# A convolutional attention block with linear attention and routed experts: where the output bias is added, where the experts' row comparisons and the routing exponentials are queued, and one branch

## The chip, the cores and the metric

The kernel runs on one core of one Trainium2 chip, all in float32 except where the profile says otherwise. The metric is the time of one execution on the device, in microseconds (us); less is better. TensorE is called PE, VectorE DVE, ScalarE ACT, GpSimd POOL and SyncE SP, as in the profile. PEld is the weight load of PE, which lies beside the matmuls.

## What is computed

The input `x` has the shape 2 x 256 x 56 x 56: two images, 256 channels (C). There are two layers, each with residual sums. Layer 1 works on 6272 tokens, which are 49 blocks of 128; block 24 holds the end of image 0 and the beginning of image 1.

```python
x = x + conv_attention(group_norm(x))       # layer 0: 1x1 conv to q,k,v; depthwise 3x3;
                                            # 7x7 neighbourhood attention, dilation 1 and 2; projection
t = tokens(x)                               # layer 1
t = t + linear_attention(layer_norm(t))     # below
t = t + experts(layer_norm(t))              # below
out = images(t)

# linear attention of tokens x
Q, K = elu(x @ Wq) + 1, elu(x @ Wk) + 1
KV = einsum('nshd,nshv->nhdv', K, x @ Wv)
msg = einsum('nlhd,nhdv,nlh->nlhv', Q, KV, Z) @ Wm          # Z: one over Q times the sum of K
h = relu(concat(x, layer_norm(msg, g1, b1)) @ W1) @ W2
return x + layer_norm(h, g2, b2)                            # b2 is the output bias of the change

# experts: top 2 of 8, hidden width 1024
probs = softmax(x @ Wr + br);  top_p, top_idx = top_k(probs, 2)
weights = top_p / top_p.sum()
y_e = gelu((norm(x) * ln_g[e] + ln_b[e]) @ W1[e] + b1[e]) @ W2[e] + b2[e]
return sum of weights * y_e over the two chosen experts
```

## The kernel before, in words

**Stages.** (1) Attention of image 0 and the convolutions. (2) The linear attention of the first half of the tokens (`linear(..., 0)`): first the stage of the keys (`keys`, L267), pair of blocks by pair of blocks, then queries, messages (`message`, L1906), feed-forward and routing (`route`, L2028) of the groups of four blocks, which run about 530 to 745 us from the start; convolution work for image 1 fills in. (3) Attention of image 1 (`Attention`, L606), with the first expert tiles run beside it, about 765 to 1030 us. (4) The linear attention of the second half (`linear(..., 1)`), with expert tiles up to number 13 beside it, to about 1440 us. (5) The remaining full expert tiles and five half tiles, to about 1970 us. (6) The last tokens are read back, transposed and written.

**Experts.** The router scatters every token's row of 256 values, with its index and its two weights, into a DRAM buffer `xs`, sorted by expert (`scatter`, L168, an indirect DMA of POOL). A tile is 256 rows of one expert. `fetch` (L1534) reads the tile's rows into `xr` and the expert's weights into `w1e` and `w2e`, and works out four small DVE results from the rows: `eq` (L1557, which row is in use; L1560 and L1561 make it the row's weight) and `idi` (L1559, the row's token as an integer); `so` and `sv` (L1563, L1567) come from the expert's number alone. `turn` (L1570) transposes the rows with PE (`px`), scales them on DVE (`xe`, L1579) and prepares `yt`, the expert's bias times the weight, on POOL (L1589). `run` (L1591) is a generator: it fetches tile t+1, does the eight hidden parts of tile t (matmuls `ph` L1607, Gelu on ACT L1611), calls `turn` for tile t+1, does the second matmuls `py` (L1625), adds them to `yt` (L1631, DVE, with `eq`) and scatters `yt` into `y` by `idi`. Each `next` of the generator is a step; the other stages place the steps between their own work.

**What sets the order.** PE's order is written out by hand: it is the order of the program (`manual_schedule`). The orders of all other engines and of the DMA queues are made by a planner before the kernel runs. It simulates the kernel and gives each engine, when it comes free, the instruction of highest priority whose inputs it takes as there; the priority is the place in the program, unless `high_priority` is given. `tc.issue_after(ins)` puts what is written under it behind `ins` on that engine. The engines execute their streams in the order planned.

**The lines that the change and the prediction touch.** `keys`: the tokens `t` of a pair are normalised into `xt` (which goes to PE), then `t` is overwritten on ACT by its scaled form (L296), and POOL adds the output bias `b2` in place (L299, 128 x 512); `t` is not read again until the feed-forward's residual. `rstd` (L257) computes a reciprocal square root with DVE L261 and POOL `pow` L262, at high priority; `message` calls it for every two blocks. `weights` (L2018): the `Exp` of the routing (L2021), then DVE lines L2022 to L2026. It is called by `route` after the matmuls L2083 and L2084, which count how many rows each expert has had and take `chosen` (L2074) and `before` (L2076) from DVE. Attention: the scores `s_ps` (L651), their Exp on ACT (L655), the product with the bias table on DVE (`p`, L656), the values `po` on PE (L665). In the second half the string list `parts` (L2303) orders the steps row by row; `e` is one expert step, and it does nothing once tile 13 is done. L2389 to L2395: `ex.more` says whether an expert has more tiles than are provided for; then the code in `If` runs. The last reads are L2340, by SP and ACT, the transposes `pto` L2352, and L2406 to L2413 are a branch to a general version, not taken here.

Of the kernel before, what the change touches and what calls it, by code (L numbers as in the profile page):

```python
# [13 lines left out]
F32 = mybir.dt.float32  # L14
AF = mybir.ActivationFunctionType
# [30 lines left out]
E = 8  # L46
# [80 lines left out]
def hybrid_kernel(ctx: ExitStack, tc: tile.TileContext, a: dict, out: bass.AP):  # L127
# [49 lines left out]
    newest = [None, None, None]  # L177
# [89 lines left out]
    def keys(tk, wk, sm, ps, bank, w_k, b2, kx, acc, n0, n, p, first, last, eager):  # L267
# [31 lines left out]
        nc.gpsimd.tensor_tensor(t, t, b2[p].unsqueeze(1).to_broadcast([rows, n, C]), ALU.add)  # L299
# [1054 lines left out]
    class Experts:  # L1354
# [179 lines left out]
        def fetch(self, t, nh, pools):  # L1534
# [20 lines left out]
            x.eq = self.small.tile([P, 2], F32, name="eq")  # L1555
            eq = x.eq[:, :nh]
            nc.vector.tensor_scalar(eq, xr[:, :, C + 3], tab.etm[:, k : k + 1], None, ALU.is_equal)  # L1557
            x.idi = self.small.tile([P, 2], mybir.dt.int32, name="idi", bufs=4)
            nc.vector.tensor_copy(x.idi[:, :nh], xr[:, :, C])  # L1559
            nc.vector.tensor_tensor(eq, eq, xr[:, :, C + 2], ALU.mult)  # L1560
            nc.vector.tensor_tensor(eq, eq, xr[:, :, C + 1], ALU.add)  # L1561
# [6 lines left out]
            return x  # L1568

        def turn(self, x, pools):  # L1570
# [7 lines left out]
            for ct in range(2):  # L1578
                newest[0] = nc.vector.tensor_scalar(  # L1579
                    x.xe[:, ct, :], px[:, ct, :nh, :].rearrange("p j t -> p (j t)"),  # L1580
                    x.sv[:, ct : ct + 1], x.sv[:, 2 + ct : 3 + ct], ALU.mult, ALU.add,
                ).ins
            b2 = pools.b2e()
# [7 lines left out]
        def run(self, ts, pools, between=lambda i: None):  # L1591
# [7 lines left out]
            for i, (t, nh) in enumerate(ts):  # L1599
# [4 lines left out]
                for j in range(NJ):  # L1604
                    p1 = pools.ph()[:, : nh * P]
                    for ct in range(2):
                        nc.tensor.matmul(  # L1607
                            p1, x.w1[:, ct, j * P : (j + 1) * P], x.xe[:, ct, :],
                            start=(ct == 0), stop=(ct == 1),
                        )  # L1610
                    nc.scalar.activation(hT[:, j, :], p1, AF.Gelu, bias=x.sv[:, 4 + j : 5 + j])  # L1611
                    if j % 2:
                        yield
# [33 lines left out]
    def linear(ph, tk, half, behind=None):  # L1647
# [258 lines left out]
        def message(n0, n, qz, out):  # L1906
# [3 lines left out]
            for k0 in range(0, n, 2):  # L1910
                pm = ps_h.tile([P, 2, C], F32, name="pm", tag="h")
# [106 lines left out]
        def weights(rt, ms, row, n):  # L2018

            r = rt.sm.tile([P, 4], F32, name="rsum")[:, :n]  # L2020
            nc.scalar.activation(ms[1], ms[1], AF.Exp)  # L2021
# [95 lines left out]
        def all_keys():  # L2117
# [58 lines left out]
    def layer1(whole, tk, conv_ctx=None, conv=None, behind=None):  # L2176
# [3 lines left out]
        conv = conv or none  # L2180

# [66 lines left out]
        def experts():  # L2248
# [7 lines left out]
            turn=lambda: tc.issue_after(newest[1]),  # L2256
            xr=lambda: xc.tile([P, 2, XW], F32, name="xr"),
# [27 lines left out]
        with ExitStack() as ph:  # L2285
            ln = linear(ph, tk, 1)
            pools.px = lambda: ln.ps_a.tile([P, 2, 2, P], F32, name="px", tag="a")
# [6 lines left out]
            with tc.manual_schedule(engines={mybir.EngineType.PE}):  # L2294
                for i, _ in enumerate(ln.keys()):
# [11 lines left out]
                    "fefepefefereePfePeree", "eepeereePeePeree", "eeepePe",  # L2307
# [7 lines left out]
        with ExitStack() as ph:  # L2315
# [10 lines left out]
                turn=nullcontext,  # L2326
                xr=lambda: xp.tile([P, 2, XW], F32, name="xr"),
# [56 lines left out]
            with tc.manual_schedule(engines={mybir.EngineType.PE}):  # L2384
# [15 lines left out]
    with ExitStack() as ph:  # L2400
# [6 lines left out]
        bad[0:1, 0:1], min_val=0, max_val=1, skip_runtime_bounds_check_because="a comparison's result"  # L2407
# [42 lines left out]
```

## Time and profile before

| what | value |
|---|---|
| median of 3 runs | 1992.35 us (1986.69 to 1992.89) |
| the profiled execution's own time | 1992.68 us |
| its span, first to last instruction | 1990.9 us |
| PE busy | 1840.8 us (92%) |
| DVE / ACT / POOL busy | 1092.3 / 705.9 / 584.9 us |
| mean granted PE clock | 0.970 |

All times of the trace count from the start of the span; 1.8 us of the execution's own time lie outside it. A line of the timeline gives the start, the duration, the engine, the line of the kernel, the operation, its output and inputs with their shape, the number of instructions put together, and in brackets how long the engine had been idle before it and what released it. A line of the windows gives a stretch, its length, the busy time and number of instructions of PE, PEld, DVE, ACT and POOL, the granted PE clock, the busy share of the DMA engines and GB/s.

### The profile page before, as it was taken

The numbers are of one execution on the slowest core, as the hardware profiler recorded it, in microseconds if no ns is written. First come the engines' busy times: TensorE is split into PE (matmuls) and PEld (weight loads), VectorE is DVE, ScalarE is ACT, GpSimd is POOL, SyncE is SP. The second block draws the span as 40 slices with busy tenths as digits, with TensorE's granted clock in tenths as the row PEclk, the third lists the DMA queues.
The fourth block names the chain that finished last, engine by engine and source line by source line (L and its number), as shares of the span: only waits on it lengthen the run. The fifth ranks groups of instructions, "written<-read, shape, count | busy, mean of one in ns | idle before, by whom it ended". The sixth has DMA issues, their size and how long they took to land.

```text
span 1990.9 us, 27720 instructions
## 1 busy us (share of the span) xinstructions
PE 1840.8 (92%) x9996; PEld 1306.9 (66%) x9996; DVE 1092.3 (55%) x2727; ACT 705.9 (35%) x1337; POOL 584.9 (29%) x634
## 2 busy tenths in 40 slices
PE   6999899988899997999989989999899999999996
PEld 3544454556555654666668756577788888888885
DVE  6887988889897646465547334555532212121221
ACT  2333324334433323545536443323322222323332
POOL 4630132025102344111126311445422222222221
PEclk9999899999999995999999999999999999999998
DMA  4753422350014235664474110115477676767995
GB/s 113 158 131 114 141 86 80 93 167 17 25 43 111 84 86 179 161 160 125 130 199 130 56 35 32 50 59 150 147 227 201 190 199 190 199 190 196 297 282 164
DMA packets 200152, 268.85 MB, mean 135 GB/s; under 512 B 30952, under 2 KB 158614, under 8 KB 199760
## 3 DMA queue, kind: packets, MB, share of 16 engines
q1 hardware_dynamic: 167920, 223.95, 37.6%
q0 software_dynamic: 19728, 27.54, 7.5%
q10 hardware_dynamic: 12352, 15.43, 2.3%
q8 instruction: 83, 1.36, 0.3%
q14 instruction: 69, 0.57, 0.1%
HBM read 200.19 MB, written 70.95 MB: 136 GB/s over the span
## 4 chain that ended last, share of the span: by engine, by line
PE 49%; DMA 4%; DVE 3%; ACT 3%; issue 1%; POOL 1%; SPq 0%; ACTq 0%; DVEq 0%; POOLq 0%
PE py L1625 13%; PE ph L1607 13%; PE p L1946 4%; PE x L1625 2%; PE x L1607 2%; DMA y<-yt,idi 2%; PE py L1962 2%; PE po L665 2%; DMA xr<-xs 1%; PE pm L1916 1%; PE kx L316 1%; PE x L358 1%; PE kp L304 1%; PE s_ps L651 1%; PE pq L1876 1%; PE px L1576 1%
## 5 line engine op out<-in xcount | busy, mean ns | idle before, releaser
L1607 PE MATMUL ph<-xe,w1e 128*128 128x256 f32 (+1 forms) x1448 | 311.3, 371 | 12.8 <-ACT hT L1611 7.9
L1625 PE MATMUL py<-w2e,hT 128*128 128x256 f32 x1392 | 311.4, 380 | 0.0
L1611 ACT ACTIVATE hT<-ph,sv 128x256 f32<-128x256 f32 (+1 forms) x362 | 165.6, 462 | 390.1 <-PE ph L1607 377.3
L1607 PEld LDWEIGHTS ph<-xe,w1e 128*128 128x128 f32 x1448 | 262.7, 191 | 52.0 <-ACT hT L1611 10.1
L1625 PEld LDWEIGHTS py<-w2e,hT 128*128 128x128 f32 x1392 | 260.3, 190 | 33.0 <-issue 0.2
L168 POOL DMA_INDIRECT y<-yt,idi x101 | 160.2, 1587 | 326.7 <-DVE yt L1631 188.7
L578 DVE SCALAR_TENSOR_TENSOR yc<-ypad,w,yc 128x1120 f32<-128x1120 f32 x144 | 202.5, 1410 | 28.4 <-ACT yc L568 26.0
L262 POOL TENSOR_TENSOR rs<-rs,mhalf 128x2 f32<-128x2 f32 (+3 forms) x90 | 72.8, 812 | 324.1 <-DVE rs L261 276.0
L528 PE MATMUL py<-x_sb,wq 128*128 128x448 f32 (+1 forms) x384 | 154.2, 533 | 7.2 <-ACT ypad L534 5.6
L655 ACT ACTIVATE p<-s_ps 112x952 f32<-112x952 f32 (+5 forms) x88 | 102.1, 1160 | 150.6 <-PE s_ps L651 101.4
L1559 DVE CAST idi<-xr 128x2 int32<-128x2 f32 (+1 forms) x53 | 10.1, 191 | 255.1 <-DMA xr<-xs 255.1
L656 DVE TENSOR_TENSOR p<-p,tab 112x952 f32<-112x952 f32 (+5 forms) x88 | 122.0, 1389 | 48.6 <-ACT p L655 41.3
L549 PE MATMUL pc<-ypad,diag 128*128 128x448 f32 x324 | 131.4, 547 | 0.0
L1631 DVE SCALAR_TENSOR_TENSOR yt<-py,eq,yt 128x256 f32<-128x256 f32 x87 | 41.8, 482 | 156.6 <-PE py L1625 156.5
L1589 POOL TENSOR_SCALAR yt<-b2e,eq 128x256 f32<-128x256 f32 x101 | 52.2, 522 | 253.5 <-DMA b2e<-in_L_ffn_b 214.9
L168 POOL DMA_INDIRECT xs<-row,si x98 | 97.5, 995 | 70.2 <-DVE si L2092 40.2
L528 PEld LDWEIGHTS py<-x_sb,wq 128*128 128x128 f32 x384 | 71.7, 197 | 69.4 <-issue 55.5
L571 DVE SCALAR_TENSOR_TENSOR yc<-ypad,w,yc 128x784 f32<-128x784 f32 x96 | 104.9, 1113 | 1.3 <-ACT yc L568 0.9
L665 PE MATMUL po<-p,v 98*32 98x170 f32 (+5 forms) x960 | 71.1, 378 | 30.3 <-DVE p L656 15.5
L549 PEld LDWEIGHTS pc<-ypad,diag 128*128 128x128 f32 x324 | 60.0, 191 | 52.3 <-issue 48.5
L1946 PE MATMUL p<-m2T,fw 128*128 128x512 f32 (+2 forms) x224 | 93.8, 542 | 0.0
L1946 PE MATMUL p<-xT,fw 128*128 128x512 f32 (+1 forms) x208 | 92.7, 568 | 0.0
(392 smaller groups left out, 2889.0 us busy)
## 6 DMA issues: line engine op xcount, KB each, us to landing
w1e<-in_L_ffn_W SPq DMA_DIRECT2D x53, 1024.0 KB
w2e<-in_L_ffn_W SPq DMA_DIRECT2D x53, 1024.0 KB
yd<-yc SPq DMA_DIRECT2D x24, 784.0 KB
ld<-yd SPq DMA_DIRECT2D x28, 448.0 KB
xr<-xs SPq DMA_DIRECT2D x48, 260.0 KB
b2e<-in_L_ffn_b SPq DMA_DIRECT2D x53, 128.0 KB
t<-td SPq DMA_DIRECT2D x12, 512.0 KB
y<-t ACTq DMA_DIRECT2D x24, 256.0 KB
```

Of the source, the lines that this page charges most:

```text
L168: ins = nc.gpsimd.indirect_dma_start(out=dst[:, :], out_offset=bass.IndirectOffsetOnAxis(ap=index, axis=0), in_=src, in_offset=None, **kw,)
L528: nc.tensor.matmul(py[:, :n, :], self.wq1[:, ct, oc * P : (oc + 1) * P], self.x_sb[:, ct, (q0 + g0) * WW : (q0 + g0 + n) * WW], start=(ct ...
L549: nc.tensor.matmul(pc, diag[:, tap, :], ypad[:, dy : dy + SHARE, dx : dx + WW], start=(tap == 0), stop=(tap == 8),)
L571: nc.vector.scalar_tensor_tensor(yc[:, y0:y1, :], src, w, yc[:, y0:y1, :], ALU.mult, ALU.add)
L578: nc.vector.scalar_tensor_tensor(yc[:, y0:y1, :], src, w, yc[:, y0:y1, :], ALU.mult, ALU.add)
L655: nc.scalar.activation(p[:nk, :, :n], s_ps[:nk, :, :n], AF.Exp)
L656: nc.vector.tensor_tensor(grid(p), grid(p), table[:nk], ALU.mult)
L665: nc.tensor.matmul(dst[hs] if w is None else den[hs], v[:nk, hs] if w is None else w[:nk, :], p[:, h, :, o : o + q.shape[2]], start=first ...
L1607: nc.tensor.matmul(p1, x.w1[:, ct, j * P : (j + 1) * P], x.xe[:, ct, :], start=(ct == 0), stop=(ct == 1),)
L1611: nc.scalar.activation(hT[:, j, :], p1, AF.Gelu, bias=x.sv[:, 4 + j : 5 + j])
L1625: nc.tensor.matmul(py, hT[:, j, h * P : (h + 1) * P], x.w2[:, j, :], start=(j == 0), stop=(j == NJ - 1),)
L1946: nc.tensor.matmul(p1[:, :w], fw1[:, k, oc * P : (oc + 1) * P], rhs, start=(k == 0), stop=(k == 3))
```

## The change

Five edits. (1) `keys` gets no bias for the full pairs of the first half, so 12 of its 24 POOL additions of 128 x 512 leave it; `message` in the first half adds the bias instead, at the head of each pass over two blocks. The single block 24 keeps its addition in `keys`. (2) The four DVE lines that need `xr` become `weigh`; for tiles fetched while `pools.beside` is true (the attention of image 1) it is called in `turn`, after `xe`, and otherwise in `fetch` as before. (3) The last Gelu written so far is remembered, and in the second half the Exp of `weights` is queued behind it on ACT. (4) The last two strings of `parts` get one and two letters `e` more at their head. (5) In the ordinary run the `If` on `more`, with its code, is gone; `more` is merged into `bad` with one DVE operation, so the general version would take care of it.

```diff
--- before.py
+++ after.py
@@ -174,7 +174,7 @@
 
     evac_n = [0]
 
-    newest = [None, None, None]
+    newest = [None, None, None, None]
 
     def evac(dst, src):
 
@@ -296,7 +296,8 @@
             nc.scalar.activation(
                 t[:, k, :], t[:, k, :], AF.Identity, bias=up[:, 1, k : k + 1], scale=up[:, 0, k : k + 1]
             )
-        nc.gpsimd.tensor_tensor(t, t, b2[p].unsqueeze(1).to_broadcast([rows, n, C]), ALU.add)
+        if b2 is not None:
+            nc.gpsimd.tensor_tensor(t, t, b2[p].unsqueeze(1).to_broadcast([rows, n, C]), ALU.add)
         yield
         kps = bank()[p]
         for k in range(n):
@@ -1552,20 +1553,27 @@
                 x.w2, a["L1_ffn_W2"][bass.ds(e, 1)].rearrange("one (j p) d -> p (one j) d", p=P)
             )
             x.e = e
+            x.etm, x.eq = tab.etm[:, k : k + 1], None
+            if not pools.beside:
+                self.weigh(x)
+            so = self.small.tile([P, 4 + NJ, E], F32, name="so")
+            nc.vector.tensor_tensor(
+                so, self.sel, tab.oh[:, k, :].unsqueeze(1).to_broadcast([P, 4 + NJ, E]), ALU.mult
+            )
+            x.sv = self.small.tile([P, 4 + NJ], F32, name="sv")
+            nc.vector.tensor_reduce(x.sv, so, AX.X, ALU.add)
+            return x
+
+        def weigh(self, x):
+
+            xr, nh = x.xr, x.nh
             x.eq = self.small.tile([P, 2], F32, name="eq")
             eq = x.eq[:, :nh]
-            nc.vector.tensor_scalar(eq, xr[:, :, C + 3], tab.etm[:, k : k + 1], None, ALU.is_equal)
+            nc.vector.tensor_scalar(eq, xr[:, :, C + 3], x.etm, None, ALU.is_equal)
             x.idi = self.small.tile([P, 2], mybir.dt.int32, name="idi", bufs=4)
             nc.vector.tensor_copy(x.idi[:, :nh], xr[:, :, C])
             nc.vector.tensor_tensor(eq, eq, xr[:, :, C + 2], ALU.mult)
             nc.vector.tensor_tensor(eq, eq, xr[:, :, C + 1], ALU.add)
-            so = self.small.tile([P, 4 + NJ, E], F32, name="so")
-            nc.vector.tensor_tensor(
-                so, self.sel, tab.oh[:, k, :].unsqueeze(1).to_broadcast([P, 4 + NJ, E]), ALU.mult
-            )
-            x.sv = self.small.tile([P, 4 + NJ], F32, name="sv")
-            nc.vector.tensor_reduce(x.sv, so, AX.X, ALU.add)
-            return x
 
         def turn(self, x, pools):
 
@@ -1580,6 +1588,8 @@
                     x.xe[:, ct, :], px[:, ct, :nh, :].rearrange("p j t -> p (j t)"),
                     x.sv[:, ct : ct + 1], x.sv[:, 2 + ct : 3 + ct], ALU.mult, ALU.add,
                 ).ins
+            if x.eq is None:
+                self.weigh(x)
             b2 = pools.b2e()
             nc.sync.dma_start(
                 b2, a["L1_ffn_b2"][bass.ds(x.e, 1)].rearrange("one d -> (one d)").partition_broadcast(P)
@@ -1608,7 +1618,9 @@
                             p1, x.w1[:, ct, j * P : (j + 1) * P], x.xe[:, ct, :],
                             start=(ct == 0), stop=(ct == 1),
                         )
-                    nc.scalar.activation(hT[:, j, :], p1, AF.Gelu, bias=x.sv[:, 4 + j : 5 + j])
+                    newest[3] = nc.scalar.activation(
+                        hT[:, j, :], p1, AF.Gelu, bias=x.sv[:, 4 + j : 5 + j]
+                    ).ins
                     if j % 2:
                         yield
                 between(i)
@@ -1908,6 +1920,9 @@
             mns = []
             ss = sm.tile([P, 4], F32, name="ssm")
             for k0 in range(0, n, 2):
+                if half == 0:
+                    tt = tk.at(n0 + k0, 2)
+                    nc.gpsimd.tensor_tensor(tt, tt, b2.unsqueeze(1).to_broadcast([P, 2, C]), ALU.add)
                 pm = ps_h.tile([P, 2, C], F32, name="pm", tag="h")
                 for k in range(min(2, n - k0)):
                     for b, c0, c1 in parts(n0, n):
@@ -2018,7 +2033,8 @@
         def weights(rt, ms, row, n):
 
             r = rt.sm.tile([P, 4], F32, name="rsum")[:, :n]
-            nc.scalar.activation(ms[1], ms[1], AF.Exp)
+            with tc.issue_after(newest[3]) if half and newest[3] is not None else nullcontext():
+                nc.scalar.activation(ms[1], ms[1], AF.Exp)
             nc.vector.tensor_scalar(r, ms[1], 1.0, None, ALU.add)
             nc.vector.reciprocal(r, r)
             nc.vector.tensor_tensor(row[:, :n, C + 1], ms[1], r, ALU.mult)
@@ -2126,7 +2142,7 @@
                     j = i - k
                     if j == i and j < len(pairs):
                         live[j] = keys(
-                            tk, wk, sm, ps_a, bank, w_k, b2, kx, acc, *pairs[j], j == 0, j == len(pairs) - 1, j < 3 and half == 0
+                            tk, wk, sm, ps_a, bank, w_k, b2 if half or pairs[j][1] == 1 else None, kx, acc, *pairs[j], j == 0, j == len(pairs) - 1, j < 3 and half == 0
                         )
                     if 0 <= j < len(pairs):
                         next(live[j])
@@ -2178,6 +2194,7 @@
 
         run = tk.run
         conv = conv or none
+        newest[3] = None
 
         def fill(n=1):
             for _ in range(n):
@@ -2254,6 +2271,7 @@
         xc = experts() if run else None
         pools = SimpleNamespace(
             turn=lambda: tc.issue_after(newest[1]),
+            beside=run == 0,
             xr=lambda: xc.tile([P, 2, XW], F32, name="xr"),
             xe=lambda: xc.tile([P, 2, ST], F32, name="xe"),
             yt=lambda: xc.tile([P, 2, C], F32, name="yt"),
@@ -2284,6 +2302,7 @@
 
         with ExitStack() as ph:
             ln = linear(ph, tk, 1)
+            pools.beside = False
             pools.px = lambda: ln.ps_a.tile([P, 2, 2, P], F32, name="px", tag="a")
             pools.ph = lambda: ln.ps_q.tile([P, 2, ST], F32, name="ph", tag="q")[:, 0, :]
             summed = []
@@ -2304,7 +2323,7 @@
                     "qewexewexqwexqq", "meqemeq", "meqfmqfeffff",
                     "mqfpPPPPfmqfrfrff", "mqfpPPPPfmqfrfrff", "mqfpPPPPfmqfrfrff",
                     "mqfpcfmfqrfPPfPrPef", "meqefepfmfqPPrPfPerefe", "mefefpfmferePPfePerPee",
-                    "fefepefefereePfePeree", "eepeereePeePeree", "eeepePe",
+                    "fefepefefereePfePeree", "eeepeereePeePeree", "eeeeepePe",
                 )
                 for part in steps(ln, order[early1:], parts, {"e": tiles, "w": merging, "x": prepared}):
                     if part == "c":
@@ -2324,6 +2343,7 @@
             ps_t = ph.enter_context(tc.tile_pool(name="p4pt", bufs=2, space=PSUM, reuse_waits="tile"))
             pools = SimpleNamespace(
                 turn=nullcontext,
+                beside=False,
                 xr=lambda: xp.tile([P, 2, XW], F32, name="xr"),
                 xe=lambda: xp.tile([P, 2, ST], F32, name="xe"),
                 yt=lambda: xp.tile([P, 2, C], F32, name="yt"),
@@ -2386,13 +2406,16 @@
                 for i, _ in enumerate(ex.run(slots, pools, between)):
                     for _ in range((i > 2) + (2 < i < 12)):
                         chunk(work)
-            more = nc.values_load(
-                ex.more[0:1, 0:1], min_val=0, max_val=NTL,
-                skip_runtime_bounds_check_because="the number of tiles is bounded by the counts",
-            )
-            with tc.If(more > 0):
-                for _ in ex.run([(t, 2) for t in range(NFS, NTL)] + [(k, 1) for k in range(NHS, E)], pools):
-                    pass
+            if run == 0:
+                nc.vector.tensor_tensor(bad, bad, ex.more[0:1, 0:1], ALU.max)
+            else:
+                more = nc.values_load(
+                    ex.more[0:1, 0:1], min_val=0, max_val=NTL,
+                    skip_runtime_bounds_check_because="the number of tiles is bounded by the counts",
+                )
+                with tc.If(more > 0):
+                    for _ in ex.run([(t, 2) for t in range(NFS, NTL)] + [(k, 1) for k in range(NHS, E)], pools):
+                        pass
             last = [read(n0, n, False) for n0, n in order[early2:]]
             for h in held + last:
                 write(*h, (nc.scalar, nc.sync), [(ps_t, "pt"), (ps_h, "ph")])
@@ -2404,7 +2427,8 @@
         rest = first_image(conv, ph)
         layer1(ph, tokens, conv_ctx, rest, anchors["residual4"])
     bad = nc.values_load(
-        bad[0:1, 0:1], min_val=0, max_val=1, skip_runtime_bounds_check_because="a comparison's result"
+        bad[0:1, 0:1], min_val=0, max_val=NTL,
+        skip_runtime_bounds_check_because="a comparison's result or a number of tiles",
     )
     with tc.If(bad > 0):
         with ExitStack() as ph:
```

More of the change, by code (lines that the diff above doesn't have):

```diff
@@ L1554, in fetch @@
             x.e = e
[L1555 to L1561, printed above, removed]
+            x.etm, x.eq = tab.etm[:, k : k + 1], None
+            if not pools.beside:
+                self.weigh(x)
             so = self.small.tile([P, 4 + NJ, E], F32, name="so")
@@ L1568, in fetch @@
             return x
+        def weigh(self, x):
+            xr, nh = x.xr, x.nh
+            x.eq = self.small.tile([P, 2], F32, name="eq")
+            eq = x.eq[:, :nh]
+            nc.vector.tensor_scalar(eq, xr[:, :, C + 3], x.etm, None, ALU.is_equal)
+            x.idi = self.small.tile([P, 2], mybir.dt.int32, name="idi", bufs=4)
+            nc.vector.tensor_copy(x.idi[:, :nh], xr[:, :, C])
+            nc.vector.tensor_tensor(eq, eq, xr[:, :, C + 2], ALU.mult)
+            nc.vector.tensor_tensor(eq, eq, xr[:, :, C + 1], ALU.add)
         def turn(self, x, pools):
```

## The prediction

> **What bounds the kernel now.** I read the totals first, then the slices, then the stretches by stage, then the stalls of PE one by one.
>
> ```profile
> PE 1840.8 (92%) x9996; PEld 1306.9 (66%) x9996; DVE 1092.3 (55%) x2727; ACT 705.9 (35%) x1337; POOL 584.9 (29%) x634
> PE   6999899988899997999989989999899999999996
> PEclk9999899999999995999999999999999999999998
> ```
>
> PE is idle for only 1990.9 - 1840.8 = 150 us, so no removal of work on DVE, ACT or POOL is worth its busy time; it is worth the PE stall that it ends. The clock row has one dark place, slice 16 (747 to 796 us).
>
> ```profile
> 600.00:700.00 100.00, 97.98 (x369) 58.51 (x368) 69.03 (x258) 36.40 (x99) 31.32 (x36) 1.00 0.37 92
> 750.00:775.00 25.00, 22.59 (x163) 13.87 (x162) 19.14 (x92) 9.44 (x23) 13.97 (x14) 0.51 0.44 127
> 775.00:800.00 25.00, 17.26 (x126) 9.84 (x119) 9.86 (x26) 9.18 (x13) 6.91 (x9) 0.73 0.75 243
> 1375.00:1400.00 25.00, 18.85 (x90) 15.32 (x89) 9.64 (x52) 7.42 (x17) 12.19 (x13) 0.91 0.42 117
> 1440.00:1955.00 515.00, 512.70 (x2532) 452.16 (x2531) 115.43 (x414) 146.45 (x315) 144.55 (x141) 1.00 0.76 218
> ```
>
> The last stage is PE back to back (512.70 of 515 us) at full clock with DMA at 0.76. So whatever time PE saves before 1440 us reaches the end whole. The message and query stage (600:700) is bound by PE too. The two rows around 775 and the one at 1375 hold stalls that the change speaks of.
>
> **What the Trainium skill says.** "TensorE: Matmul & The Clock Gate", Part 1: after an idle window of some 3.4 us PE runs at half rate for a while. The trace agrees: `po` of 112x238 takes 0.61 us at 776 and 1.02 us at 829.81, after an idle time; the clock record is at half from 1395.5 to 1402.4 us after the idle 5.81 us at 1397. "ScalarE: Activation LUTs", What ACT_TABLE_LOAD costs: 1283 ns a load; here each takes 1.28 us. "GPSIMD Engine Reference", 1. Specifications: POOL shares SBUF interfaces with DVE. The trace agrees: during POOL's bias additions DVE's L294 takes 1.23 us, otherwise 0.15. No page prices a wait of one of these engines on another's result; those come from the trace.
>
> **Edit 3, the Exp behind the Gelus.**
>
> ```profile
> 1389.90 1.28 ACT L2021 ACT_TABLE_LOAD   x1
> 1395.76 0.20 ACT L2021 ACTIVATE m<-m 128x2 f32<-128x2 f32 x1 [4.58 <-DVE m L2080]
> 1395.98 1.28 ACT L1611 ACT_TABLE_LOAD   x1
> 1397.80 2.08 PE L1607 MATMUL ph<-xe,w1e 128*128 128x256 f32 x4 [5.81 <-ACT hT L1611]
> 1404.03 0.29 PE L2083 MATMUL pp<-chosen,tri 128*128 128x16 f32 x2
> ```
>
> ACT runs in order. At 1389.90 it has done five of tile 12's eight Gelus and turns to the Exp of row 9, which waits 4.58 us for DVE; DVE itself waited 4.71 us for a POOL `pow` behind scatters. Three Gelus stand behind the Exp, PE behind them for 5.81 us, and then it runs at half clock for 6.9 us, which loses 3.45. Row 9's `weights` is written after the matmul L2083, and all `ph` of tile 12 are ahead of that in PE's order, so the newest Gelu is tile 12's eighth. With the Exp behind it, PE would come to L2083 at 1404.03 - 5.81 - 3.45 = 1394.8, where `before` (DVE L2076, ending 1397.24) is late next: it goes on at 1397.3, **6.7 us sooner**. Against this stand reloads of the Gelu table: the Exp now ends a tile, so tile 13's Gelus begin with a load, 1.28 us, and likewise tile 12's because row 8's Exp (1358.60, now mid tile 11) moves behind tile 11's eighth Gelu (1366.6). Tile 12's lies before the 2.5 us in which PE waits for DVE anyway; of tile 13's I count 1.0 us, since PE waits for its first Gelus. Row 8's row weights come 8 us later, but their scatters start at 1384.36: covered; without that cover PE would meet it as a late `pow`, below. Other rows' Exps either share a table state with the linear attention's own Exps or already follow the Gelus. Net **-5.7 us**; bounds -8 (both reloads hidden, the clock clean) and +1.3 (the stall stays, one reload added).
>
> **Edit 2, the comparisons at the turn.** These lines show what it aims at.
>
> ```profile
> 782.97 0.23 DVE L1557 TENSOR_SCALAR eq<-xr,etmA 128x2 f32<-128x2 f32 x1 [5.72 <-DMA xr<-xs]
> 785.12 1.16 PE L665 MATMUL po<-p,v 112*32 112x280 f32 x8 [6.78 <-DVE p L656]
> 827.78 0.17 DVE L1559 CAST idi<-xr 128x2 int32<-128x2 f32 x1 [6.24 <-DMA xr<-xs]
> 829.81 1.02 PE L665 MATMUL po<-p,v 112*32 112x238 f32 x8 [2.98 <-issue]
> 881.73 0.99 DVE L1579 TENSOR_SCALAR xe<-x,sv 128x256 f32<-128x256 f32 x2
> ```
>
> DVE stands at `eq` or `idi` until the rows land, with `p` behind it, for which PE waits. If the four lines really moved behind `xe`: the first `po` could go at 778.7, but the next in PE's order is the transpose of the same rows, landed at 782.9, so 787.14 becomes 783.1, 4.0 us; at 829.81 2.98 us of stall and about 2.5 of half clock. That is **-9.5 us**; the other blocks of DVE (5.25 us at 878, 2.5 at 983, 3.6 at 1006) stand beside a busy PE. But does the place in the program move them? The cast at 827.78 belongs to tile 3 (fourth read of rows, fourth cast), whose `xe` is at 881.73 and whose `fetch` is written after tile 2's turn, `xe` at 854.52. So it already runs 27 us ahead of its place in the program, and ahead of `p` at 828.57, which is written earlier and has the higher priority. The planner put it there because its simulation had the rows landed and DVE free, and neither changes: no `issue_after` is given. In the first stall also `p` is written before the first fetch. **I take 0**, bounds -10.5 and +3 (a reshuffled cast before another `p`, one stall as at 829.81). What it adds is nothing: the same four DVE lines, 0.73 us a tile. `yt` L1589 and the scatter need `eq` and `idi`; after `xe` there are 10 us or more until the first L1631.
>
> **Edit 1, the bias with the messages.**
>
> ```profile
> 492.57 1.27 POOL L299 TENSOR_TENSOR t<-t,b 128x512 f32<-128x512 f32 x1 [2.55 <-ACT t L296]
> 536.35 1.42 POOL L262 TENSOR_TENSOR rs<-rs,mhalf 128x2 f32<-128x2 f32 x1 [24.64 <-DVE rs L261]
> ```
>
> Twelve additions of 1.27 us leave the keys and come back, 15.2 us of POOL either way. In the keys stage DVE is nearly full, and the additions slow it: over all twelve the DVE instructions beside them take about 10.6 us more than their like elsewhere. Were they gone from there, up to 10 us could come back. But here as well the planner sets the place: the addition starts as soon as ACT has written `t`, as at 492.57, in POOL's gaps; a lower priority doesn't lengthen the queue in front of it. And those that do move find POOL idle for 24.64 us before 536.35. **I take 0**; bounds -10 and +4 (three additions ahead of a `pow` on the path).
>
> **Edits 4 and 5.** The steps: tiles need 114, the attention takes 61, the keys 15, rows 0 to 9 the next 36, so they run out in row 10, and letters added in row 11 find nothing: 0. One added in row 10 brings a step forward by less than its own length: 0. The branch:
>
> ```profile
> 1968.22 1.55 POOL L168 DMA_INDIRECT y<-yt,idi  x1 [6.31 <-DVE yt L1631]
> 1973.21 2.37 SPq L2340 DMA_DIRECT2D yr<-y  x4
> 1978.25 5.16 PE L2352 MATMUL pto<-ident,yr 128*128 128x128 f32 x26 [10.88 <-DMA yr<-y]
> ```
>
> The last reads start at 1973.21, some 1.2 us after the last scatter's landing at 1972.0 is seen, because POOL first closes the branch (0.85 us from 1972.33). Without it they wait for the scatter alone: **-1.2 us**, bounds 0 and -2.5. The branches of the other engines lie under the scatter's landing. The last branch, on `bad`, stays; "Runtime: NRT & Kernel Launch", Instruction fetch mechanics, says that a taken branch outside the fetched pages stalls, and that remains. The merging is one small DVE operation before a wait of 10.88 us.
>
> **Sum.** -5.7 + 0 + 0 + 0 - 1.2 = -6.9 us. Against the profiled execution's 1992.68 that is 1985.8; the median stands 0.3 us under it, so **1985.5 us**.
>
> **Rivals.**
> - *The comparisons do move* (chance 0.25): -6.9 - 9.5 = -16.4, 1976 us. For it: the stalls are real, and small shifts in the simulated times may carry a cast past a `p`. Against it: the cast that runs ahead of its program place.
> - *A stall only changes its releaser* (0.18): the Exp leaves, but the late `pow` stays and each of rows 8 to 10 pays its reload on PE's path: -6.7 + 3 x 1.28 + about 1 of half clock = -1.8, with the branch -3.0: 1989.5 us. That edits 1, 2 and 4 do nothing at all is contained here and in my forecast.
> - *Slower* (0.17): an Exp tied behind a Gelu makes the row's scatters late, and a `pow` is queued behind them on POOL, as in the 4.71 us of 1392. The message's or next row's chain then stops PE: about 5 us idle and 3.45 of half clock, 8.5 us a time. One such stall (-6.9 + 8.5) brings it even, two decide: +10, 2002 us. For it: this POOL queue is already late once. Against it: the planner sees the tie and orders POOL by it.
>
> **Chances.** My forecast has 0.40. About 0.3%, 6 us, is what a measurement of this kernel can tell from no change. Of the forecast's own spread (-11 to -3) two thirds lie beyond 6 us: 0.27; with 0.25 of the first rival and 0.03 of the second, faster is 0.55. Same: 0.13 + 0.15 = 0.28. Slower: 0.17. The range takes in the first rival with some of edit 1's relief (1973), and ends at 1996, one surplus stall: it leaves out the two-stall case and the extreme of edits 1 and 2 together.
>
> **What would show it.** Right: the Exp of row 9 after tile 12's last Gelu, no 5.81 us ahead of `ph`, L2083 some 6.7 us sooner against 1375; the last reads starting 3.8 us after the last scatter begins, not 5.0; `idi` still waiting for `xr` ahead of `p` near 780 and 828, and bias additions still before 510 us. Wrong: casts right behind `xe` and a clean clock at 775:800 (first rival), new ACT loads ahead of PE's stalls (second), a `pow` behind scatters with PE idle (third).

## The result and the profile after

The changed kernel takes 1984.67 us (median of 12 runs, 1978.55 to 1988.47) where the kernel before takes 1989.89 us (12 runs on the same chip, 1981.81 to 1996.06): a ratio of 0.997, 95% interval 0.9956 to 0.9985. That is 3.0 to 8.8 us less; 6.9 had been forecast. The spans of the two profiled executions are 1990.9 and 1983.8 us.

The head of the page:

```profile
span 1983.8 us, 27692 instructions
PE 1840.1 (93%) x9996; PEld 1304.7 (66%) x9996; DVE 1093.3 (55%) x2728; ACT 705.8 (36%) x1337; POOL 578.8 (29%) x634
PEclk9999999999989996999999999999999999999998
```

PE does the same work in less idle time, and the dark place of the clock near slice 16 is still there. The stretches by time (busy us of PE, PEld, DVE, ACT and POOL, then the PE clock, DMA share and GB/s):

```profile
750.00:775.00 25.00, 21.20 (x140) 13.56 (x140) 18.14 (x100) 9.86 (x26) 12.82 (x13) 0.51 0.43 124
775.00:800.00 25.00, 17.28 (x126) 9.59 (x123) 13.20 (x42) 7.63 (x12) 9.55 (x12) 0.67 0.70 239
1375.00:1400.00 25.00, 23.39 (x126) 20.53 (x125) 11.30 (x63) 8.38 (x18) 12.25 (x13) 1.00 0.52 154
```

Around 775 us the stall is still there: 17.28 us of PE after, 17.26 before. At 1375 us PE has 23.39 us where it had 18.85, and the clock is full.

Row 9's Exp and its surroundings, from the timelines of ACT and PE:

```profile
1391.82 0.47 ACT L1621 ACTIVATE hT<-ph,sv 128x256 f32<-128x256 f32 x1 [0.39 <-PE ph L1617]
1392.31 1.28 ACT L2037 ACT_TABLE_LOAD   x1
1393.61 0.20 ACT L2037 ACTIVATE m<-m 128x2 f32<-128x2 f32 x1
1385.44 3.72 PE L1617 MATMUL ph<-xe,w1e 128*128 128x256 f32 x16 [1.61 <-ACT hT L1621]
1389.89 1.89 PE L1617 MATMUL ph<-xe,w1e 128*128 128x256 f32 x8
1394.68 0.29 PE L2099 MATMUL pp<-chosen,tri 128*128 128x16 f32 x2
1405.78 2.00 PE L1617 MATMUL ph<-xe,w1e 128*128 128x256 f32 x8 [1.04 <-ACT hT L1621]
```

The start of tile 12 in the kernel before:

```profile
1386.51 3.72 PE L1607 MATMUL ph<-xe,w1e 128*128 128x256 f32 x16 [0.33 <-ACT hT L1611]
```

The Exp follows the eighth Gelu of the tile (1391.82), and PE does not stand behind it. The idle 5.81 us ahead of `ph` are gone; 1.61 us (before: 0.33) and 1.04 us have come at the starts of tiles 12 and 13, where the Gelu table is loaded again. The kernel has as many table loads as before, 58: the tie moves them from the middle of a tile to its start.

The comparisons in the attention of image 1, from the timelines of DVE and PE:

```profile
786.37 0.23 DVE L1572 TENSOR_SCALAR eq<-xr,etmA 128x2 f32<-128x2 f32 x1 [5.72 <-DMA xr<-xs]
829.53 0.17 DVE L1574 CAST idi<-xr 128x2 int32<-128x2 f32 x1 [4.59 <-DMA xr<-xs]
788.51 1.16 PE L666 MATMUL po<-p,v 112*32 112x280 f32 x8 [6.77 <-DVE p L657]
```

Both waits stand where they stood, ahead of the same `p`. The first is 5.72 us to the hundredth, with PE idle for 6.77 us. The second is shorter in this execution, 4.59 us where it was 6.24; PE is idle for 1.33 us where it was 2.98, and no half clock follows. This is not put down to the edit: in the kernel with edits 1, 2 and 4 (below) this wait is 6.05 us, with PE idle for 2.79. Nor have the bias additions moved in time. The view of their new line says that all twelve run from 435.8 to 500.3 us, inside the stage of the keys, as before:

```profile
L1925 POOL TENSOR_TENSOR t<-t,b x12: 1252/1266/1362, 435.8 to 500.3; 128x512 f32<-128x512 f32 x12
```

The end:

```profile
1961.73 1.55 POOL L168 DMA_INDIRECT y<-yt,idi  x1 [6.31 <-DVE yt L1643]
1965.51 2.36 SPq L2360 DMA_DIRECT2D yr<-y  x4
1970.14 5.78 PE L2372 MATMUL pto<-ident,yr 128*128 128x128 f32 x26 [9.26 <-DMA yr<-y]
```

The last reads start 3.78 us after the last scatter begins (before 4.99), and PE is idle 9.26 us (before 10.88). From the start of this scatter to the end of the span it is 22.0 us, where it was 22.7.

**The same matmul in two traces.** PE does the same 9996 matmuls in the same order in all these kernels, so the start of one matmul can be set beside its start in the other trace. This table has the difference to the kernel before in us (negative is sooner), at matmuls that start there at the times given. It separates the stages, which a total can't: two executions of one program also differ by some us in where PE runs at half clock.

| matmul at, in before | 428 | 502 | 748 | 840 | 1045 | 1178 | 1384 | 1414 | 1900 | 1978 |
|---|---|---|---|---|---|---|---|---|---|---|
| changed kernel | +1.60 | +0.62 | +3.39 | -0.21 | -0.09 | -1.71 | -2.34 | -8.15 | -6.49 | -8.11 |
| edit 3 alone | -0.02 | -0.10 | +0.13 | -4.50 | -2.69 | +0.22 | -0.31 | -6.12 | -6.04 | -6.00 |
| edit 5 alone | +1.22 | +1.11 | +1.21 | +2.53 | +3.07 | +3.79 | +3.20 | +3.92 | +5.27 | +3.54 |
| edits 1, 2 and 4 | -3.02 | -3.02 | -2.79 | -5.45 | -4.97 | -6.17 | -6.59 | -6.05 | -6.92 | -6.66 |

The step from 1384 to 1414 is -5.81 in the two kernels with edit 3 and within 0.8 of nothing in the others; the step from 1900 to 1978 is -1.62 and -1.73 in the two with edit 5, and within 0.3 of nothing in the others. This second step does not reach the end of the span whole. There the changed kernel is 7.1 us ahead of the kernel before, where it was 8.11 ahead at 1978; edit 5 alone is 5.4 us behind, where it was 3.54 behind.

### The profile page after: what moved, and what is told of

It is laid out like the page before. It is cut to its first block, busy times and chain, and to the rows that moved or that the text cites. A ratio compares the mean times of both kernels' runs of the same rounds, so it can differ in the third digit from the quotient of the medians.

```text
span 1983.8 us, 27692 instructions
## 1 busy us (share of the span) xinstructions
PE 1840.1 (93%) x9996; PEld 1304.7 (66%) x9996; DVE 1093.3 (55%) x2728; ACT 705.8 (36%) x1337; POOL 578.8 (29%) x634
## 3 DMA queue, kind: packets, MB, share of 16 engines
q8 instruction: 81, 1.33, 0.3%
## 4 chain that ended last, share of the span: by engine, by line
PE 48%; DMA 5%; DVE 3%; ACT 3%; issue 1%; SPq 0%; POOL 0%; ACTq 0%; DVEq 0%; POOLq 0%
PE ph L1617 13%; PE py L1637 13%; PE p L1961 4%; DMA xr<-xs 2%; PE x L1637 2%; PE py L1977 2%; PE x L1617 2%; DMA xs<-in_c_fill 2%; PE po L666 2%; PE pm L1931 1%; PE kx L317 1%; PE x L359 1%; PE kp L305 1%; PE pq L1888 1%; PE px L1584 1%; PE s_ps L652 1%
## 5 line engine op out<-in xcount | busy, mean ns | idle before, releaser
L572 DVE SCALAR_TENSOR_TENSOR yc<-ypad,w,yc 128x784 f32<-128x784 f32 x96 | 104.9, 1114 | 1.3 <-ACT yc L569 0.9
```

The source lines that it names most:

```text
L572: nc.vector.scalar_tensor_tensor(yc[:, y0:y1, :], src, w, yc[:, y0:y1, :], ALU.mult, ALU.add)
```

## Experiments

Times are compared by the ratio to the kernel before on the same chip. That took 1990.68 us beside edit 3 alone, edit 5 alone, edits 1, 2 and 4 and the tied comparisons; 2002.73 beside the two kernels of the stall of tile 12, the bias in a block and both ties; and 1991.44 beside the last three. The intervals of two ratios together leave a difference of two kernels uncertain by about 5 us either way. Where a gain is read by the same matmul, it is that of one execution.

### Edit 3 alone

The lines that remember the newest Gelu are left out here.

```diff
-            nc.scalar.activation(ms[1], ms[1], AF.Exp)
+            with tc.issue_after(newest[3]) if half and newest[3] is not None else nullcontext():
+                nc.scalar.activation(ms[1], ms[1], AF.Exp)
```

> The kernel before with edit 3 alone (the second half's Exp queued behind the newest Gelu). Theory (the gain is this tie, plus the branch): 5 to 6 us less than before; no idle time of 5.8 us ahead of ph in tile 12, the stretch 1375 to 1400 us some 4 us fuller on PE, the Exp of row 9 after tile 12's eighth Gelu, and one reload of 1.28 us seen as a PE stall at the start of tile 12 or 13 each. Rival (the gain comes from the edits in the first half and the attention, the tie only trades the stall for reloads): within 2 us of before.

1984.07 us against 1990.68, ratio 0.9968 (0.9953 to 0.9982): by itself as much as the whole change. The reloads show at both tiles:

```profile
1387.47 3.72 PE L1607 MATMUL ph<-xe,w1e 128*128 128x256 f32 x16 [1.61 <-ACT hT L1611]
1396.71 0.29 PE L2086 MATMUL pp<-chosen,tri 128*128 128x16 f32 x2
1407.81 2.00 PE L1607 MATMUL ph<-xe,w1e 128*128 128x256 f32 x8 [1.04 <-ACT hT L1611]
```

### Edit 5 alone

Shortened; the wider bound of the last branch's value is left out.

```diff
-            more = nc.values_load(ex.more[0:1, 0:1], ...)
-            with tc.If(more > 0):
-                for _ in ex.run(...): pass
+            nc.vector.tensor_tensor(bad, bad, ex.more[0:1, 0:1], ALU.max)
```

> The kernel before with edit 5 alone (no branch on more, which is merged into bad). Theory: 1.2 to 1.6 us less, too little for the times to tell; in the profile the last reads start 3.8 us after the last scatter begins, where before they started 5.0 us after, and PE is idle some 9.3 us ahead of the last transposes instead of 10.9. Rival (branches on five engines cost a stop of their own, or the planner uses the longer block to reorder the last stage): 3 us or more less, with a gap of under 8 us ahead of the last transposes.

1989.95 us, ratio 0.9998 (0.9986 to 1.001): too little for the times, as expected. From the last scatter to the last reads 1973.49 to 1977.23 is 3.74 us, PE's gap is 9.15 us, and the step in the table is -1.73 us. But from the scatter to the end of the span it is 22.8 us, no less than before. Over all the traces it is 22.65 to 24.05 us in the four kernels with the branch and 21.64 to 23.63 in the nine without it. So edit 5 starts the last transposes sooner; that it shortens the execution isn't shown.

### Edits 1, 2 and 4

```diff
-            with tc.issue_after(newest[3]) if half and newest[3] is not None else nullcontext():
-                nc.scalar.activation(ms[1], ms[1], AF.Exp)
+            nc.scalar.activation(ms[1], ms[1], AF.Exp)
```

and the branch put back.

> The changed kernel without edits 3 and 5, so the bias with the messages, the comparisons at the turn and the letters alone. Theory: within 1 us of before; eq still waits some 5.7 us for the rows near 783 us and idi some 5 to 6 us near 828 us, ahead of p, and the bias additions of the first half still run between 430 and 505 us. Rival (these edits carry part of the gain): 3 us or more less than before, with at least one of the two waits gone from ahead of p.

1990.57 us, ratio 1.0005 (0.9991 to 1.0019). The waits: 6.69 us at `eq` (778.07) and 6.05 us at `idi` (822.38), ahead of `p`; the additions run from 431.0 to 496.7 us. The traces agree with this: PE, DVE, ACT, POOL and SP execute the same instructions in the same order in this kernel as in the kernel before. So its 6.66 us in the table are what two executions of the same streams can differ by, and edits 1, 2 and 4 are moves on paper. Likewise the streams of the changed kernel differ from those of edit 3 alone only by the branch and its merging.

### The stall of tile 12: wait or table load

In the kernel before and in the changed one the routing weights of the second half are left out: a copy takes the place of the Exp, and no table is loaded for it. Each was run once, and only the traces are read.

```diff
-            nc.scalar.activation(ms[1], ms[1], AF.Exp)
+            nc.scalar.activation(ms[1], ms[1], AF.Identity if half else AF.Exp)
```

> The kernel before, with the second half's Exp of the routing weights replaced by a copy with the identity function at the same place on ACT; the weights of the second half are then wrong, all else is computed. No table load stands at it. Theory (the stall of tile 12 is the wait in ACT's order, the loads are a part): PE's idle time ahead of ph in tile 12 falls from 5.8 by one load to 4.3 to 4.8 us, and the copy waits some 5.9 us for DVE. Rival (the table loads make the stall): under 1.5 us of idle time there.

In the kernel before, from the timelines of ACT and PE:

```profile
1404.75 0.20 ACT L2021 ACTIVATE m<-m 128x2 f32<-128x2 f32 x1 [5.90 <-DVE m L2080]
1405.37 2.08 PE L1607 MATMUL ph<-xe,w1e 128*128 128x256 f32 x4 [4.42 <-ACT hT L1611]
```

Without a table load there 4.42 of the 5.81 us remain, and ACT waits 5.90 us for DVE. The stall was the place of the Exp in ACT's order; the load was 1.4 us of it.

> The changed kernel with the same replacement (identity for the Exp of the second half's weights, so these weights are wrong). It prices the reloads that the tie adds: Theory: the idle times of 1.61 us and 1.04 us of PE ahead of ph at tiles 12 and 13 fall to about 0.3 and 0, so that PE passes the stretch from 1350 us to tile 14 some 2.3 us sooner than in the changed kernel. Rival (the reloads lie beside other waits): under 0.7 us.

In the changed kernel the idle time at tile 12 is 0.33 us instead of 1.61, and at tile 13 there is none instead of 1.04: the reloads make up 1.28 + 1.04 = 2.3 us of PE's idle time, as stated. In exchange 0.54 us came ahead of L2099, where `chosen` is late next, so that 1.8 us are what they cost:

```profile
1397.81 3.72 PE L1617 MATMUL ph<-xe,w1e 128*128 128x256 f32 x16 [0.33 <-ACT hT L1621]
1407.74 0.37 PE L2099 MATMUL pp<-chosen,tri 128*128 128x16 f32 x2 [0.54 <-DVE chosen L2090]
```

### The comparisons really moved

```diff
             if x.eq is None:
-                self.weigh(x)
+                with tc.issue_after(newest[0]):
+                    self.weigh(x)
```

> The changed kernel with one thing added: the comparisons of the attention's tiles are queued on DVE behind their tile's xe, so that they really move. First rival of the prediction: 9.5 us less than the changed kernel (4.0 at the first stall, 3.0 and 2.5 of half clock at the second), with no wait for the rows on DVE ahead of p. Theory of a changed releaser: DVE goes on, but PE's next instruction, the transpose of the same rows, waits for their landing instead, and the clock stays low near 780: 2 to 5 us less. A cost: eq later makes yt on POOL late and with it L1643; then no gain, and PE waits for yt after py.

1976.0 us against 1990.68, ratio 0.9941 (0.9921 to 0.9961). Against the changed kernel's 0.997 that is 0.0029, or 5.8 us less. No instruction of DVE waits for rows any more between 750 and 1035 us. PE's own rows show what came instead at the first stall:

```profile
773.79 0.68 PE L666 MATMUL po<-p,v 112*32 112x280 f32 x8 [0.53 <-DVE p L657]
778.93 1.09 PE L1584 MATMUL x<-ident,xr 128*128 128x128 f32 x4 [3.99 <-DMA xr<-xs]
783.25 3.56 PE L1618 MATMUL x<-xe,w1e 128*128 128x256 f32 x8 [2.15 <-DMA w1e<-in_L_ffn_W]
```

Of 6.77 us 0.53 are left at `po`, but the transpose waits 3.99 us for the rows and `ph` 2.15 us for the weights. The cost that was expected, PE waiting for a late `yt`, isn't there. By the same matmul, PE gains 3.9 us against the changed kernel from 775 to 840 us, over both stalls. But that execution of the changed kernel had a short second stall. Against the kernel before the gain is 10.1 us from 748 to 840, and the three kernels without the tie on this chip and the changed kernel lie between 1.3 us behind and 4.6 ahead in that stretch. So the tie gains about 5 to 11 us there, in an execution that is the shortest of ten (1971.32 us; five took 1971 to 1974 us, five 1978 to 1985). By the times the gain of 5.8 us lies between the two expectations. From 1000 to 1045 us this execution gains another 3.3 us, in idle time and half clock. That is not put down to the tie: of the two other kernels with it one gains 3.3 and one 1.4 there, and the bias in a block, without it, 1.6.

### The bias additions really moved, in a block

```diff
+        newest[4] = nc.gpsimd.tensor_tensor(acc[p, :n, :], acc[p, :n, :], ks[:, :n, :], ALU.add).ins
...
+                    with tc.issue_after(newest[4]):
+                        nc.gpsimd.tensor_tensor(tt, tt, b2.unsqueeze(1).to_broadcast([P, 2, C]), ALU.add)
```

> The changed kernel with one thing added: the bias additions of the first half are queued on POOL behind the last accumulation of the keys, so that they really leave the stage of the keys and run in POOL's idle time before the first message. It tests the bound of edit 1: DVE's instructions beside the additions took 10.6 us more than their like. If DVE's time is the stage's limit: 5 to 10 us less than the changed kernel, PE passing the first message some 5 to 10 us sooner relative to the start of the keys. Rival (the stage waits on a chain through POOL, ACT and PE as much as on DVE, or other POOL work slows DVE as well): 0 to 3 us less. Slower case: the additions delay the first pow at about 536 us; then 1 to 4 us more.

Ratio 0.9969 (0.9954 to 0.9983; 1995.77 us against 2002.73): nothing beside the changed kernel's 0.997. The table of the same matmul tells why, here as the difference to the changed kernel at matmuls that start there at the given times:

| matmul at, in the changed kernel | 428 | 494 | 518 | 545 | 690 |
|---|---|---|---|---|---|
| bias in a block | -1.05 | -12.34 | -2.59 | +0.95 | -1.58 |
| bias spread (below) | -6.44 | -17.81 | -18.21 | -17.48 | -14.38 |
| no bias (below) | -6.48 | -18.15 | -18.56 | -18.56 | -21.10 |
| kernel before | -1.59 | -2.09 | -0.61 | -0.62 | -3.39 |

The last row is the kernel before, whose streams are the same as the changed kernel's here. It gains 2.8 us from 545 to 690, and eight other kernels gain 2.5 to 2.7: the changed kernel's own execution lost time there, its clock at 0.86 from 545 to 570 and 0.94 from 570 to 600 us, where the kernel before had 0.93 and 1.00.

With the bias in a block the keys gain 11.3 us; 9.8 of them are lost at once, from 494 to 518, and more than the rest by 545. From the timelines of POOL, DVE and PE:

```profile
499.54 14.68 POOL L1926 TENSOR_TENSOR t<-t,b 128x512 f32<-128x512 f32 x12
497.97 17.09 DVE L572 SCALAR_TENSOR_TENSOR yc<-ypad,w,yc 128x784 f32<-128x784 f32 x2
515.59 0.14 DVE L336 COPY kc<-pk 128x2 f32<-128x2 f32 x1
515.72 1.11 PE L1849 MATMUL kxt<-ident,kxs 128*128 128x128 f32 x4 [9.99 <-DVE kc L336]
```

Two instructions of DVE that take 2.44 us at this place in the changed kernel take 17.09 us, the whole block of POOL's additions long; `kc` stands behind them, and PE behind `kc`.

### Both ties

> The changed kernel with both ties: the attention's comparisons behind their xe, the first half's bias additions behind the keys. The sum of the two kernels with one tie each if they touch different stages: casts alone gave about 6 us less than the changed kernel, the bias alone 0 to 10; so 6 to 16 us less, 1969 to 1979 us. Rival: as in the two kernels with one tie each, a stall removed early only meets another wait later; then no better than the casts alone.

Ratio 0.9936 (0.9914 to 0.9958; 1989.26 us against 2002.73), beside 0.9941 for the comparisons alone: the block of additions brings nothing here either. In the traces of this chip the first stall of the attention lies elsewhere: PE is idle for 4.1 us at an earlier `po` (789.76) with the bias in a block, and for 4.2 (788.43) with both ties, so there the tied comparisons did not end it.

### The bias additions spread over the messages

```diff
                 rs = rstd(sm, ss[:, k0 : k0 + kn], 1.0 / C)
+                if half == 0:
+                    tt = tk.at(n0 + k0, 2)
+                    with tc.issue_after(newest[1]):
+                        nc.gpsimd.tensor_tensor(tt, tt, b2.unsqueeze(1).to_broadcast([P, 2, C]), ALU.add)
```

> The changed kernel, but each bias addition of the first half is queued on POOL behind the pow of its own message (two blocks), so that the twelve are spread over the message stage, 530 to 700 us, instead of one block behind the keys. Theory (the additions stop DVE while they run; behind the keys twelve in a row stopped it for 14.7 us on PE's path, spread out each stops it about 1.3 us beside a PE that is busy 98%): the keys keep the 11 us that they gained in the kernel with the block, PE loses up to 3 us in the message stage; 7 to 11 us less than the changed kernel. Rival (the message chain DVE, POOL, ACT, PE is as tight as the keys'): the gain is given back in the message stage, within 3 us of the changed kernel.

Ratio 0.9933 (0.9911 to 0.9955; 1978.44 us against 1991.44), 7.4 us less than the changed kernel by the ratios. The keys gain 11.4 us as in the block; from 518 to 690 us 3.8 are given back against the changed kernel, and 6.4 to 6.6 if one allows for what that kernel's own execution lost there. One addition stands behind one `pow`:

```profile
545.14 1.42 POOL L262 TENSOR_TENSOR rs<-rs,mhalf 128x2 f32<-128x2 f32 x1 [20.01 <-DVE rs L261]
546.53 1.53 POOL L1939 TENSOR_TENSOR t<-t,b 128x512 f32<-128x512 f32 x1
549.06 1.42 POOL L262 TENSOR_TENSOR rs<-rs,mhalf 128x2 f32<-128x2 f32 x1 [0.99 <-DVE rs L261]
```

PE does stop for some of them. The same matmul with the bias spread, and without it (next kernel):

```profile
599.48 2.07 PE L1897 MATMUL pd<-qz,ksm 128*128 128x512 f32 x2 [2.68 <-DVE m2T L185]
595.25 1.12 PE L1897 MATMUL pd<-qz,ksm 128*128 128x512 f32 x2 [0.80 <-DVE m2T L185]
```

Beside the kernel without additions, this one loses 5.5 us from 500 to 603 us, where six of the twelve stand and PE is busy 89%, and 0.85 us from there to 740, where the other six stand and PE is busy 96%.

### No bias additions

```diff
-                if half == 0:
-                    tt = tk.at(n0 + k0, 2)
-                    nc.gpsimd.tensor_tensor(tt, tt, b2.unsqueeze(1).to_broadcast([P, 2, C]), ALU.add)
```

> The changed kernel without the twelve bias additions of the first half (the output bias of these tokens is left out; the rest is computed). The most that moving them can bring. Theory: 10 to 13 us less than the changed kernel, all of it between 430 and 500 us. Rival (what the keys gain is waited away before the messages, at the closing of the keys): under 4 us less.

Ratio 0.9903 (0.9878 to 0.9928; 1970.32 us against 1991.44), 13.3 us less than the changed kernel. The keys account for 11.7 us, and that is all of it: the 2.5 us from 518 to 690 in the table are those that the changed kernel lost by half clock, as above. So the expectation was right in the place too.

### Comparisons and spread bias together

> The changed kernel with the comparisons of the attention's tiles tied behind their xe and the bias additions tied behind the pow of their message. If the two gains lie in different stages they add: 6 us of the casts and 7 to 11 us of the bias, 13 to 17 us less than the changed kernel, a ratio to the kernel before of 0.988 to 0.991. Rival: the casts' gain depends on where the rows' landing meets the attention, and earlier messages only make the rows' transfer meet other traffic; then 7 to 11 us, ratio 0.992 to 0.994.

Ratio 0.9887 (0.9863 to 0.9911): 1967.82 us against 1991.44, the fastest kernel of the study that computes everything, and 16.5 us less than the changed kernel by the ratios. By the same matmul, against the changed kernel: -10.8 us in the keys, +3.7 in the messages, -4.2 from 775 to 840, -3.3 from 1000 to 1045; the middle two are to be read with the reservations above. 16.5 us lie in the 13 to 17 of the sum and above the 7 to 11 of the rival, so the gains add.

## Why the prediction was right

- **Edit 3, -5.7 us.** Measured -5.8 from 1384 to 1414 us, in the changed kernel and alone. The mechanism is the one forecast, but two terms were misread. In the kernel before, two windows and one line of DVE:

```profile
1395.50:1397.80 2.30, 0.00 (x0) 0.00 (x1) 1.94 (x12) 2.01 (x4) 0.94 (x2) 0.51 0.00 0
1397.80:1402.40 4.60, 4.60 (x17) 4.24 (x18) 0.79 (x5) 1.41 (x4) 0.00 (x0) 0.50 0.27 72
1396.13 0.26 DVE L2074 TENSOR_TENSOR chosen<-oh,oh 128x16 f32<-128x16 f32 x1
```

  The half clock lasts 6.9 us, but in 2.3 of these PE is idle, so it costs half of 4.6, 2.3 us, and not 3.45. And L2083 takes `chosen`, there at 1396.39; `before` (1397.24) is for L2084, behind it. So without the stall PE would come at 1404.03 - 5.81 - 2.3 = 1395.9 and wait 0.5 us, where 2.5 had been counted: most of tile 12's reload of 1.28 us shows after all. The runs agree. With edit 3 alone the matmul comes at 1396.71 without a wait, 7.0 us sooner if the 0.31 us are taken off by which that execution was ahead already (forecast 6.7); without the reload it waits 0.54 us. Tile 13's reload was put at 1.0 and took 1.04. That the errors cancel is luck.
- **Edit 2, 0.** Right: the executed order is the same, whatever the place in the program, and an explicit edge moved it. The reason given, that the planner's simulation has the rows landed and DVE free, fits this; no run shows the simulation itself.
- **Edit 1, 0.** Right for the same reason. Its bound of 10 us, what DVE loses beside POOL's additions, was close to what the keys gain once they leave: 11.3 to 11.7 us in the three kernels of the table, 9.9 with both ties and 10.8 in the last kernel.
- **Edit 4, 0.** Nothing in the executed streams differs.
- **Edit 5, -1.2.** The last reads do start 1.2 us sooner behind the scatter (4.99 to 3.78), as read from POOL's closing of the branch. PE's transposes come 1.6 and 1.7 us sooner; the further 0.4 us, between reads and transposes, were not traced. But the end of the span gains 0.7 us in the changed kernel and nothing with edit 5 alone, so this term of the sum isn't shown to reach the time. The interval of edit 5 alone leaves room for it, and for none.
- **The first rival's price, -9.5,** is not refuted by the traces, but its parts are off. Its step "787.14 becomes 783.1" left out that `ph` behind the transpose needs the weights' transfer, issued 0.9 us after the rows: 2.15 us of wait. Its second stall differs from execution to execution: 2.98 us with half clock in the kernel before, 1.33 us with none in the changed one. The times give 5.8 us, and the place from 1000 to 1045 us is open.
- **The slower rival** didn't occur: the `pow` behind scatters, which holds DVE for 4.71 us, is as late as before, but lies beside PE's work now.

The remaining -2.3 us at 1384 in the changed kernel's table row come and go between 502 and 1178 us in each kernel in another way, also in those whose streams are the same there. They are not put down to any edit.

## What to carry to other kernels

Where a planner orders the streams, moving lines in the program may move nothing: look in the trace whether the instruction already runs ahead of its place, and tie it with an explicit edge if it is to move. An instruction that waits in an engine's order should stand behind the work that others wait for; see where this puts the table loads, and whether PE waits there. An elementwise stream on POOL is best taken out of the stage where DVE is the limit and dealt out singly: where PE was busy 96% six additions cost under 1 us, where it often waited for DVE six cost 5.5, and twelve in a block took back the whole gain. Before a gain is read from two traces, set a third execution of the same streams beside them; here one trace alone had 2.8 us of half clock that looked like another kernel's gain.

## What was not expected of the hardware

- A block of twelve POOL additions of 128x512 (14.68 us) held up two DVE instructions for as long as it lasted: 17.09 us instead of 2.44. The difference is the block's length, so DVE made no progress in it. A single addition lengthened such an instruction by about 1 us: 2.00 us at 493.28 in the changed kernel, beside an addition, and 1.02 at 503.86. "GPSIMD Engine Reference", 8. Key points, says that POOL shares its SBUF interfaces with DVE and contends with instructions of two SBUF inputs; these (L572) read `ypad` and `yc`, and the trace agrees.
- The length of one idle time did not decide whether PE went to half clock. The prediction cites an idle window of some 3.4 us; here half clock came after 2.98 us (829.81 in the kernel before) and after 2.38 (1026.63 in the changed kernel: the matmuls of L359 took 1.03 us instead of 0.59). The same place in the kernel before and in the changed one:

```profile
1174.54 0.70 PE L1916 MATMUL pm<-mw,qz 128*128 128x256 f32 x2 [2.42 <-DVE qz L1890]
1175.89 2.43 PE L1916 MATMUL pm<-mw,qz 128*128 128x256 f32 x10 [0.65 <-DVE qz L1890]
1171.48 0.70 PE L1931 MATMUL pm<-mw,qz 128*128 128x256 f32 x2 [2.41 <-DVE qz L1902]
1172.83 3.40 PE L1931 MATMUL pm<-mw,qz 128*128 128x256 f32 x9 [0.65 <-DVE qz L1902]
```

  The idle times differ by 0.01 us, and half clock follows only in the second. So whether a stall costs its half clock as well is no sure part of a gain.
